# A decoder layer on one core: the last chunk's dt chain and the scan's first loads are rearranged at the seam of two stages

## The chip, the cores and the metric

The kernel runs on one core of a Trainium2 chip. Its engines are TensorE (PE, with its weight loads as PEld), VectorE (DVE), ScalarE (ACT), GpSimd (POOL) and SyncE (SP, which issues most transfers). The metric is the device time of one execution in microseconds, as the median of several runs. Before the change it is 3256.49 us (three runs, 3252.81 to 3258.94).

## The reference, cut to what matters

The input x has 4 sequences of 1024 tokens with 512 features. A Mamba block comes first, then cross-attention to 64 context tokens, then a dense layer with routed low-rank experts; each is followed by a layer norm. The change touches the Mamba block alone:

```
xz = rmsnorm(x) @ in_proj_w.T;  u, z = split(xz)          # 1024 channels each
u  = silu(causal_conv(u) + conv_b)
dt_r, Bm, Cm = split(u @ x_proj_w.T, [32, 48])            # 32, 16, 16 columns
dt = softplus(dt_r @ dt_proj_w.T + dt_proj_b)
dA = exp(dt * A);  dBu = dt * Bm * u                      # 16 states per channel
h_t = dA_t * h_{t-1} + dBu_t                              # scan over the tokens
y  = sum_n(h * Cm) + u * D;  y = y * silu(z);  out = y @ out_proj_w.T
```

All arithmetic is in f32; products that need more than the fast matmul type gives are split into a high and a low part and summed from three matmuls.

## The kernel before

**Two stages and their seam.** `mamba_in` (line 354) is the input stage. It goes through 8 chunks (`NC`) of 512 tokens (`T`). In each chunk, each of 8 slots (`KI`, `slot`, line 595) handles 128 of the 1024 channels: projection to u and z, convolution, silu. What a slot starts is finished in later slots: `at(d, phase, f)` puts a function into the table `Slots` for d slots later, and each slot runs its due functions in four phases. The table `AP` (line 33) holds the delays. The results go to DRAM: `pk[c][jp][:, :, q]` holds, for a pair of channel blocks jp, the quantities dt (q = 0), dt u (q = 1), u (2) and z (3); `b` and `c` hold B and C.

`scan_mlp` (line 658) is the second stage. Its steps (`Step`, line 681) are numbered by k: one state n of 16, for one group g of 4 channel blocks of one chunk. `load` brings in dt and dt u of a pair of blocks, `load_b` one row of B copied to all partitions, `load_c` the chunk's C. `times_b` multiplies dt u by B on GpSimd (two instructions of 128x1024 per step), `exp` makes dA on ScalarE into one of two PSUM banks (tile `da`), `scan` runs the recurrence on VectorE (four per step), `turn` transposes its result on TensorE and `times_c` multiplies by C and accumulates. `quarter(k, q, other)` (line 1095) writes out a quarter of a step: it works on steps k - 1, k and k + 1 at once. For the first 40 steps no matmuls of the following MLP run beside the scan.

**The tail of the last chunk.** When the last of a chunk's `x_proj` matmuls is issued (line 525), one slot later `project` (line 546) copies the result to `pr` (dt's input) and `bc` (B and C) on ScalarE and stores B; `project_rest` makes pr's low part on VectorE. Two slots after that `turn_c` transposes `bc` into a bank of the pool `pp`, and `put_c` (line 561) copies C out of that bank, into the first columns of `bc` itself, and stores it. The eight `dt` (line 571) follow at the delays `AP["b"]`, two in every slot from two to five slots on. Each is one matmul into one of two PSUM banks (`pd`, tile `dt`); one slot later `dt_softplus` runs on ScalarE; two slots after the second of a pair `dt_u` (line 585) stores dt, multiplies it by u on GpSimd, copies the first token's dt to `dt0` (odd chunks) and stores the product.

After the last chunk (line 645) nine more slots are written out, with no new chunk in them; what is due even later is left to the generator `rest`. Then `scan_mlp` writes step 0's loads of dt and dt u, C's load and the loads of B for steps 0 and 1, all on SyncE, then step 0's products with B and its first two exps (lines 1139 to 1148). The quarters of the first four steps (`EARLY_STEPS`) follow, and each second quarter lets `rest` run one slot more. Only then are the input stage's last pools closed (`bx.close()`) and those of the early scan opened.

**What sets the order.** Each stage issues through `InOrder` (line 294), which chains each engine's instructions, SyncE excepted, in the order in which that stage writes them. The two stages have a chain each; how the two are merged on an engine, and the order of SyncE's transfers, is decided by the framework's scheduler, which reckons with a timeline of its own. ScalarE's tables for softplus and for exp differ, so an `ACT_TABLE_LOAD` is put in wherever the two follow each other. Each transfer signals one of eight counters, taken in turn over the whole program, and is issued only when the earlier transfer on the same counter has landed; that wait stands on the engine that issues it.

Of the kernel before, what the change touches and what calls it, by code (L numbers as in the profile page):

```python
# [10 lines left out]
F32 = mybir.dt.float32  # L11
# [3 lines left out]
ALU = mybir.AluOpType  # L15
AX = mybir.AxisListType
PSUM = bass.MemoryType.PSUM
DRAM = bass.MemoryType.DRAM

P = 128  # L20
# [4 lines left out]
NS = 16  # L25
DTR = 32
T = 512
NT = T // P
NC = N // T
# [3 lines left out]
AP = {  # L33
    "cv": (1, 1),
    "cw": (1, 3),
    "ut": (2, 1),
    "uu": (2, 2),
    "up": (3, 0),
    "zt": (1, 1),
    "zz": (1, 3),  # L40
    "th": (1, 0),
# [96 lines left out]
for g, first in enumerate((4, 6)):  # L138
    for n in range(1, 16):
        for t in range(4):  # L140
            i = 4 * (n - 1) + t
# [5 lines left out]
                kind = (None, JS0, AS0, JS0, None)[i % 5]  # L147
            if kind:
                kind[g].add((n, t))
EARLY_STEPS = 4  # L150
H, DK, SK = 16, 32, 64
E, R = 8, 16
ER = E * R
# [128 lines left out]
def open_pool(tc, name, bufs, **kw):  # L282
    return tc.tile_pool(name=name, bufs=bufs, reuse_waits="tile", **kw)
# [40 lines left out]
class Slots:  # L324
# [5 lines left out]
    def at(self, d, phase, f, *args):  # L330
        self.due.setdefault((self.now + d, phase), []).append(lambda: f(*args))
# [17 lines left out]
def put(nc, dr, c, jp, q, src):  # L349

    nc.sync.dma_start(dr["pk"][c][jp][:, :, q], src)


def mamba_in(tc, cn, a, dr, sx):
# [5 lines left out]
    nc = pin  # L360
    ident, pvec = cn["ident"], cn["pvec"]
    slots = Slots()
    at, run = slots.at, slots.run
    with ExitStack() as ctx:
        up = sx.enter_context(open_pool(tc, "a_u", bufs=8, side="right"))
        pd = sx.enter_context(open_pool(tc, "a_pd", bufs=2, space=PSUM, side="right"))
        wp = ctx.enter_context(open_pool(tc, "a_w", bufs=1))
        xp = ctx.enter_context(open_pool(tc, "a_x", bufs=1))
        tp = ctx.enter_context(open_pool(tc, "a_t", bufs=2))
        sm = ctx.enter_context(open_pool(tc, "a_sm", bufs=2))  # L370
        pw = ctx.enter_context(open_pool(tc, "a_pw", bufs=2))
        qp = ctx.enter_context(open_pool(tc, "a_q", bufs=1, space=PSUM))
        pp = ctx.enter_context(open_pool(tc, "a_p", bufs=5, space=PSUM))

        wu = [wp.tile([P, KD, DI], F32R, tag=f"wu{i}", name=f"wu{i}") for i in range(2)]
# [60 lines left out]
        class Step:  # L436
# [82 lines left out]
            def x_proj(self, j):  # L519
                if j == 0:  # L520
                    self.xp = qp.tile([P, T], F32, tag="xp", name="ps_xp")
                nc.tensor.matmul(
                    self.xp, wxp[:, j], self.u[j // 2][:, j % 2], start=j == 0, stop=j == KI - 1
                )
                if j == KI - 1:
                    at(1, 0, self.project)
                    at(1, 0, self.project_rest)
                    for b in range(KI):
                        at(*AP["b"][b], self.dt, b)

            def gate(self, j):

# [20 lines left out]

            def turn_c(self):

                ps = pp.tile([P, NT, P], F32, tag="mm", name="ps_c")
                for t in range(NT):
                    nc.tensor.transpose(ps[:, t], self.bc[:, t * P : (t + 1) * P], ident)
                at(0, 1, self.put_c, ps)

            def put_c(self, ps):
                ct = self.bc[:, 0 : NT * NS].rearrange("p (t n) -> p t n", n=NS)
                nc.scalar.copy(ct, ps[:, :, 112:128])
                nc.sync.dma_start(dr["c"][self.c], ct)

# [5 lines left out]
            def dt(self, j):  # L571

                jp, i = divmod(j, 2)
                if i == 0:
                    self.dts[jp] = sp.tile([P, 2, T], F32, tag="r", name="r", bufs=4)
                ps = pd.tile([P, T], F32, tag="dt", name="ps_dt")
                nc.tensor.matmul(ps, wdt[:, j * P : (j + 1) * P], self.pr, start=True, stop=True)
                at(*AP["ds"], self.dt_softplus, j, ps, self.dts[jp][:, i])
                if i:
                    at(*AP["du"], self.dt_u, jp)  # L580

            def dt_softplus(self, j, ps, r):
                nc.scalar.activation(r, ps, AF.Softplus, bias=vec(V_DTB + j))
# [1 line left out]
            def dt_u(self, jp):  # L585
                r = self.dts.pop(jp)
                put(nc, dr, self.c, jp, 0, r)
                q = sp.tile([P, 2, T], F32, tag="q", name="q", bufs=4)
                nc.gpsimd.tensor_tensor(q, r, self.u.pop(jp), ALU.mult)
                if self.c % 2:  # L590
                    dt0 = cn["dt0"][:, self.c // 2, 2 * jp : 2 * jp + 2]
                    nc.gpsimd.tensor_copy(dt0, r[:, :, 0])
                put(nc, dr, self.c, jp, 1, q)
# [26 lines left out]
        nc = tc.nc  # L620
# [16 lines left out]
        sp = sx.enter_context(open_pool(tc, "a_sp", bufs=2, side="right"))  # L637
        nc = pin
# [3 lines left out]
                    load_in(wz, DI, j // 3, [nc.gpsimd, nc.vector])  # L642
                slot(c, j)
        assert not later
        for n in range(9):
            slot(NC, n)

    def rest():
        n = 9
        while slots.due:  # L650
            slot(NC, n)
            n += 1
            yield
# [4 lines left out]
def scan_mlp(tc, cn, a, dr, before, bx, then):  # L658
# [5 lines left out]
    nc = pin  # L664
    ident = cn["ident"]
    GJ = 4
    with ExitStack() as ctx, ExitStack() as sx:
# [6 lines left out]
        pd = sx.enter_context(open_pool(tc, "b_pd", bufs=2, space=PSUM))  # L674
# [6 lines left out]
        class Step:  # L681
# [7 lines left out]
                self.by_add, self.by_turn = (AS0[self.g], JS0[self.g]) if self.g < 2 else (AS, JS)  # L689
                self.da = {}  # L690

            def load(self, jp, q):

                pk = pks[self.g, jp, q] = kp.tile([P, 2, T], F32, tag=f"pk{q}", name=f"pk{q}")
                nc.sync.dma_start(pk, dr["pk"][self.c][2 * self.half + jp][:, :, q])

            def load_c(self):
                if self.half == 0:
                    cts[self.c] = bp.tile([P, NT, NS], F32, tag="c", name="c", bufs=2)
                    nc.sync.dma_start(cts[self.c], dr["c"][self.c])  # L700

            def load_b(self):
                bs[self.k] = bp.tile([P, 1, T], F32, tag="b", name="b")
                nc.sync.dma_start(
                    bs[self.k], dr["b"][self.c][self.n : self.n + 1].partition_broadcast(P)
                )

# [132 lines left out]
        def at(d, phase, f, *args):  # L840

            due.setdefault((now[0] + d, phase), []).append(lambda: f(*args))

        def run(phase):
            for f in due.pop((now[0], phase), ()):
                f()
# [241 lines left out]
        n = NC * 2 * NS  # L1088
# [3 lines left out]
        def step(k):  # L1092
            return all_steps[k] if 0 <= k < n else None

        def quarter(k, q, other):


            before, this, nxt = (step(i) for i in (k - 1, k, k + 1))
            run(0)
            if q == 0 and step(k + 2):  # L1100
                step(k + 2).load_b()
            after = step(k - k % NS + NS)
            if after and (k % NS, q) in LOADS:
                for jp, i in LOADS[k % NS, q]:
                    after.load(jp, i)
                if (k % NS, q) == (8, 0):
                    after.load_c()
            if after and not after.first and q == 0:
                if k % NS == 8:
                    after.first_decay()  # L1110
                elif k % NS == 9:
                    after.first_carry()
            if q == 1 and this and this.n == 12:
                this.load_uz(0, nc.sync)
                this.load_uz(1, nc.sync)
            if before:
                if q == 0:
                    before.carry()
                before.turn(q)
            run(1)  # L1120
            other()
            run(2)
            if this:
                this.scan(q)
            ahead = this if q < 2 else nxt
            if ahead:
                if q % 2 == 0 and not ahead.first:
                    ahead.carry_in(1 - q // 2)
                ahead.exp((q + 2) % GJ)
            if before:  # L1130
                before.times_c(q)
                if q == GJ - 1 and before.n == NS - 1:
                    before.end()
            if nxt and q < 2:
                nxt.times_b(q)
            run(3)
            now[0] += 1

        for jp in range(2):
            for i in range(2):  # L1140
                step(0).load(jp, i)
        step(0).load_c()
        for k in range(2):
            step(k).load_b()
        for jp in range(2):
            step(0).times_b(jp)
        for i in range(2):
            step(0).exp(i)
        for k in range(EARLY_STEPS):
            for q in range(GJ):  # L1150
                quarter(k, q, lambda: q % 2 or next(before, None))
        assert next(before, 0) == 0
        bx.close()
        with ExitStack() as zx:
            zps.append(zx.enter_context(open_pool(tc, "b_z", bufs=44, side="right")))
            zps.append(
                zx.enter_context(open_pool(tc, "b_zp", bufs=2, space=PSUM, side="right"))
            )
            for k in range(EARLY_STEPS, 2 * NS + 8):
                for q in range(GJ):  # L1160
                    quarter(k, q, lambda: None)
            turned[0] = 0
# [4 lines left out]
        pp = ctx.enter_context(open_pool(tc, "b_p", bufs=3, space=PSUM, side="right"))  # L1167
# [780 lines left out]
def build(tc, a, out):  # L1948
    nc = tc.nc
    with ExitStack() as ctx:  # L1950
# [39 lines left out]
        before = mamba_in(tc, cn, a, dr, bx)  # L1990
        att = Attention(tc, cn, a, dr, out)
        scan_mlp(tc, cn, a, dr, before, bx, lambda pin, mm: att.start(ctx, pin, mm))
        att.rest(ctx)
        att.run()
# [71 lines left out]
```

## Time and profile before

| what | us |
|---|---|
| median of three runs | 3256.49 |
| the profiled execution | 3250.26 |
| its span, first to last instruction | 3248.5 |
| VectorE busy in the span | 2698.2 (83%) |
| TensorE busy | 3001.8 (92%) |
| GpSimd busy | 2369.2 (73%) |
| ScalarE busy | 1973.4 (61%) |
| last matmul of the input stage's x_proj starts | 487.0 |
| first scan of step 0 | 508.08 |
| first scan of step 1 | 515.12 |

Times inside the execution count from the span's start. In a timeline, each row is one instruction or a run of equal ones: start, length, engine, source line, operation, tile written and tiles read; in brackets stands the engine's idle time just before it and what ended that time. Line 308 is the issuing line of `InOrder`, which nearly all instructions share, so the tiles' names tell them apart: `r` is dt, `q` is dt u, `hs` the state and before it the product with B, `da` the decay, `pr` and `bc` the projected values. Transfers are named by target and source in the same way.

### The profile page before, as it was taken

How to read it: one execution, taken by the hardware profiler on the slowest of the kernel's cores; microseconds unless marked ns; L12 is line 12 of the kernel's file. 1: busy time of each engine (PE TensorE's matmuls, PEld its weight loads, DVE VectorE, ACT ScalarE, POOL GpSimd, SP SyncE). 2: the span in 40 equal slices, each digit the busy share in tenths (PEclk: the TensorE clock that was granted, in tenths of full speed). 3: DMA queues.
4: the chain of work that ended last, by engine and by line, in shares of the span. 5: the costliest groups of instructions: out<-in, count | busy, mean ns of one | idle time of the engine just before them, and what ended most of it. 6: DMA issues, size and time to landing. Idle time of an engine off the chain costs nothing.

```text
span 3248.5 us, 47327 instructions
## 1 busy us (share of the span) xinstructions
PE 3001.8 (92%) x15992; PEld 2393.6 (74%) x15992; DVE 2698.2 (83%) x3836; ACT 1973.4 (61%) x3876; POOL 2369.2 (73%) x2169
## 2 busy tenths in 40 slices
PE   7999996887999999999999999999999997999987
PEld 5777773664876786786776786786785887898876
DVE  6876767997999999999999999999962346888876
ACT  3666666776666567666667666667642336666643
POOL 1334328998998999999999999999952115666664
PEclk9999995778999999999999999999999999999998
DMA  4778744336675775675765765765766432111110
GB/s 165 261 264 288 256 167 163 111 104 215 198 224 179 221 223 179 220 226 178 221 223 175 225 217 177 225 213 172 219 190 228 142 104 95 46 46 47 48 41 33
DMA packets 478472, 562.79 MB, mean 173 GB/s; under 512 B 46006, under 2 KB 309814, under 8 KB 477974
## 3 DMA queue, kind: packets, MB, share of 16 engines
q1 hardware_dynamic: 464406, 526.21, 50.6%
q10 hardware_dynamic: 13824, 33.56, 3.2%
q8 instruction: 127, 2.08, 0.3%
q14 instruction: 115, 0.94, 0.1%
HBM read 430.18 MB, written 129.50 MB: 172 GB/s over the span
## 4 chain that ended last, share of the span: by engine, by line
PE 34%; DVE 23%; POOL 12%; issue 8%; DMA 4%; ACT 3%; SPq 0%; ACTq 0%; DVEq 0%; POOLq 0%
DVE hs L308 10%; PE ps_ab L308 10%; POOL hs L308 6%; DVE acc L308 5%; PE ps_m L308 5%; PE ps_h L308 5%; PE ps_o L308 3%; PE ps_s L308 3%; PE ps_b L308 2%; POOL acc L308 2%; PE ps_y L308 2%; DVE g L308 1%; ACT da L308 1%; DMA uz<-pk 1%; DMA w<-w 1%
## 5 line engine op out<-in xcount | busy, mean ns | idle before, releaser
L308 DVE TENSOR_TENSOR_SCAN hs<-da,hs 128x512 f32<-128x512 f32 x1024 | 1214.7, 1207 | 42.7 <-ACT da L308 21.3
L308 POOL TENSOR_TENSOR hs<-pk,b 128x1024 f32<-128x1024 f32 x512 | 1217.2, 2393 | 29.7 <-issue 10.5
L308 ACT ACTIVATE da<-pk,aneg 128x512 f32<-128x512 f32 x1024 | 704.9, 689 | 554.3 <-DVE hs L308 548.6
L308 PE MATMUL ps_ab<-xn,w 128*128 128x512 f32 x3072 | 827.6, 406 | 0.0
L308 PE MATMUL ps_h<-ident,hs 128*128 128x128 f32 x4096 | 684.8, 292 | 91.0 <-DVE hs L308 47.3
L308 PEld LDWEIGHTS ps_h<-ident,hs 128*128 128x128 f32 x4096 | 535.5, 149 | 313.9 <-DVE hs L308 80.5
L308 PEld LDWEIGHTS ps_ab<-xn,w 128*128 128x128 f32 x3072 | 545.0, 189 | 95.8 <-issue 1.1
L308 PE MATMUL ps_m<-w,gs 128*128 128x512 f32 x1536 | 419.3, 408 | 9.5 <-POOL gs L308 9.5
L308 DVE SCALAR_TENSOR_TENSOR acc<-ps_h,c,acc 128x512 f32<-128x512 f32 x542 | 394.2, 727 | 37.8 <-PE ps_h L308 35.6
L308 POOL TENSOR_TENSOR acc<-acc,hc 128x512 f32<-128x512 f32 x232 | 300.1, 1293 | 52.9 <-ACT hc L308 51.5
L308 PEld LDWEIGHTS ps_m<-w,gs 128*128 128x128 f32 x1536 | 274.4, 191 | 61.7 <-POOL gs L308 14.5
L308 PE MATMUL ps_o<-wo,wy 128*128 128x512 f32 x512 | 247.8, 602 | 8.4 <-DMA wy<-y 5.1
L308 ACT ACTIVATE hc<-ps_h,c 128x512 f32<-128x512 f32 x344 | 231.3, 673 | 12.6 <-PE ps_h L308 12.5
L308 POOL TENSOR_TENSOR gs<-g,gs 128x512 fp32r<-128x512 f32 x128 | 165.8, 1295 | 85.1 <-ACT gs L308 85.1
L308 PE MATMUL ps_in<-xn,wu 128*128 128x512 f32 x768 | 214.7, 428 | 0.1
L308 POOL TENSOR_TENSOR pt<-pw,pt 128x512 fp32r<-128x512 f32 x48 | 62.7, 1306 | 194.9 <-ACT pt L308 131.2
L308 PE MATMUL ps_in<-xn,wz 128*128 128x512 f32 x768 | 191.8, 397 | 1.0 <-POOL wz L308 0.6
L308 PEld LDWEIGHTS ps_in<-xn,wu 128*128 128x128 f32 x768 | 145.3, 190 | 56.9 <-issue 22.0
L308 PEld LDWEIGHTS ps_in<-xn,wz 128*128 128x128 f32 x768 | 142.4, 188 | 34.8 <-POOL wz L308 1.1
L308 DVE SCALAR_TENSOR_TENSOR cv<-ps_in,pvec,cv 128x509 f32<-128x509 f32 (+2 forms) x192 | 143.3, 746 | 7.0 <-ACT cv L308 2.3
L308 ACT ACTIVATE hs<-hs,first 128x1 f32<-128x1 f32 x512 | 120.4, 284 | 27.1 <-POOL hs L308 11.7
L308 PEld LDWEIGHTS ps_o<-wo,wy 128*128 128x128 f32 x512 | 87.9, 194 | 66.5 <-issue 65.9
(244 smaller groups left out, 4623.9 us busy)
## 6 DMA issues: line engine op xcount, KB each, us to landing
w<-w SPq DMA_DIRECT2D x384, 512.0 KB, 5.6
b<-b SPq DMA_DIRECT2D x256, 256.0 KB, 4.1
pk<-pk SPq DMA_DIRECT2D x64, 512.0 KB, 6.7
w<-pt SPq DMA_DIRECT2D x48, 512.0 KB, 3.2
pk<-z SPq DMA_DIRECT2D x64, 256.0 KB, 2.9
pk<-u SPq DMA_DIRECT2D x32, 512.0 KB, 3.9
pk<-r SPq DMA_DIRECT2D x32, 512.0 KB, 3.1
pk<-q SPq DMA_DIRECT2D x32, 512.0 KB, 3.7
```

What stands on the lines that cost most here:

```text
L308: ins = f(*args, **kw)
```

## The change

Five things are done. The last chunk's eight dt no longer keep the delays of `AP["b"]`: pair by pair they are due in the slots two to five after `x_proj`'s end, each softplus in the same slot as its matmul and each `dt_u` in that slot as well. In the last chunk `dt_u` multiplies on VectorE instead of GpSimd; the copy to `dt0` stays on GpSimd. Step 0's loads are issued by ScalarE, B first, then dt u of both pairs, then dt of both, then B of step 1, and step 0's products with B are written directly after them, ahead of the tail; C's load stays on SyncE. Only three slots are written before the scan's pools are opened; the rest of the tail is written out in one go after the products, and the exps of step 0 and all quarters follow it, so `EARLY_STEPS` goes. C gets its own tile `ct` in every chunk instead of the first columns of `bc`, and in the last chunk its transposes use a dt bank; the pool of x_proj's bank moves to the outer stack, as it now lives longer.

```diff
-EARLY_STEPS = 4
+        qp = sx.enter_context(open_pool(tc, "a_q", bufs=1, space=PSUM, side="right"))
...
-        qp = ctx.enter_context(open_pool(tc, "a_q", bufs=1, space=PSUM))
...
-                        at(*AP["b"][b], self.dt, b)
+                        at(*(AP["b"][b] if self.c < NC - 1 else (2 + b // 2, 0)), self.dt, b)
...
-                ps = pp.tile([P, NT, P], F32, tag="mm", name="ps_c")
+                if self.c < NC - 1:
+                    ps = pp.tile([P, NT, P], F32, tag="mm", name="ps_c")
+                else:
+                    ps = pd.tile([P, NT, P], F32, tag="dt", name="ps_c")
...
-                ct = self.bc[:, 0 : NT * NS].rearrange("p (t n) -> p t n", n=NS)
+                ct = sp.tile([P, NT, NS], F32, tag="ct", name="ct", bufs=1)
...
-                at(*AP["ds"], self.dt_softplus, j, ps, self.dts[jp][:, i])
+                ds, du = (AP["ds"], AP["du"]) if self.c < NC - 1 else ((0, 1), (0, 2))
+                at(*ds, self.dt_softplus, j, ps, self.dts[jp][:, i])
                 if i:
-                    at(*AP["du"], self.dt_u, jp)
+                    at(*du, self.dt_u, jp)
...
-                nc.gpsimd.tensor_tensor(q, r, self.u.pop(jp), ALU.mult)
+                eng = nc.gpsimd if self.c < NC - 1 else nc.vector
+                eng.tensor_tensor(q, r, self.u.pop(jp), ALU.mult)
...
-        for n in range(9):
+        for n in range(3):
             slot(NC, n)
...
-        n = 9
+        n = 3
...
-            def load(self, jp, q):
+            def load(self, jp, q, eng=nc.sync):
...
-            def load_b(self):
+            def load_b(self, eng=nc.sync):
...
-        for jp in range(2):
-            for i in range(2):
-                step(0).load(jp, i)
+        step(0).load_b(nc.scalar)
+        for i in (1, 0):
+            for jp in range(2):
+                step(0).load(jp, i, nc.scalar)
+        step(1).load_b(nc.scalar)
         step(0).load_c()
-        for k in range(2):
-            step(k).load_b()
         for jp in range(2):
             step(0).times_b(jp)
+        for _ in before:
+            pass
         for i in range(2):
             step(0).exp(i)
-        for k in range(EARLY_STEPS):
-            for q in range(GJ):
-                quarter(k, q, lambda: q % 2 or next(before, None))
-        assert next(before, 0) == 0
         bx.close()
...
-            for k in range(EARLY_STEPS, 2 * NS + 8):
+            for k in range(2 * NS + 8):
```

More of the change, by code (lines that the diff above doesn't have):

```diff
@@ L690, in __init__ @@
                 self.da = {}
-            def load(self, jp, q):
+            def load(self, jp, q, eng=nc.sync):
                 pk = pks[self.g, jp, q] = kp.tile([P, 2, T], F32, tag=f"pk{q}", name=f"pk{q}")
-                nc.sync.dma_start(pk, dr["pk"][self.c][2 * self.half + jp][:, :, q])
+                eng.dma_start(pk, dr["pk"][self.c][2 * self.half + jp][:, :, q])
             def load_c(self):
@@ L700, in load_c @@
                     nc.sync.dma_start(cts[self.c], dr["c"][self.c])
-            def load_b(self):
+            def load_b(self, eng=nc.sync):
                 bs[self.k] = bp.tile([P, 1, T], F32, tag="b", name="b")
-                nc.sync.dma_start(
+                eng.dma_start(
                     bs[self.k], dr["b"][self.c][self.n : self.n + 1].partition_broadcast(P)
```

## The prediction

> **What bounds the kernel now.** I read the page's slices first: in the eighth of them (569 to 650 us and on) VectorE is full, in the seventh (487 to 569) it is not. The change touches only the seam there between two stages: the end of the input stage (last eight dt blocks) and the first steps of the scan. So I cut the span into stretches around it. Columns: stretch, its length, then busy us (and instructions) of PE, PEld, DVE, ACT, POOL, then granted clock, DMA share, GB/s.
>
> ```profile
> 490.00:500.00 10.00, 4.73 (x10) 2.43 (x10) 0.00 (x0) 5.95 (x9) 4.38 (x3) 0.50 0.99 347
> 510.00:520.00 10.00, 5.33 (x19) 3.55 (x19) 7.60 (x8) 5.84 (x12) 10.00 (x7) 0.50 0.73 259
> 520.00:530.00 10.00, 7.47 (x31) 5.70 (x30) 10.00 (x11) 6.50 (x13) 10.00 (x5) 0.50 0.16 55
> ```
>
> From 520 us VectorE and GpSimd work without a gap, and VectorE stays at 9.3 us or more of every 10 up to 740 us (one stretch of 8.3). So a shift of the point where VectorE starts to run steadily reaches the end of the stage at full size; nothing behind the seam is changed. That point is the third row of VectorE's timeline (start, length, instruction, idle before it and what ended it):
>
> ```profile
> 489.17 0.68 DVE L308 TENSOR_TENSOR pr<-ps_xp,pr 32x512 fp32r<-32x512 f32 x1 [3.26 <-ACT bc L308]
> 508.08 4.64 DVE L308 TENSOR_TENSOR_SCAN hs<-da,hs 128x512 f32<-128x512 f32 x4 [18.23 <-POOL hs L308]
> 515.12 5.84 DVE L308 TENSOR_TENSOR_SCAN hs<-da,hs 128x512 f32<-128x512 f32 x5 [2.40 <-POOL hs L308]
> ```
>
> Step 0's scans (508.08) start 18.23 us after VectorE's last work of the input stage, and step 1's (515.12) wait again for GpSimd. GpSimd's timeline says what it did:
>
> ```profile
> 503.28 2.35 POOL L308 TENSOR_TENSOR q<-r,u 128x1024 f32<-128x1024 f32 x1 [2.72 <-issue]
> 505.71 4.64 POOL L308 TENSOR_TENSOR hs<-pk,b 128x1024 f32<-128x1024 f32 x2
> 510.31 2.34 POOL L308 TENSOR_TENSOR q<-r,u 128x1024 f32<-128x1024 f32 x1
> 512.74 13.91 POOL L308 TENSOR_TENSOR hs<-pk,b 128x1024 f32<-128x1024 f32 x6
> ```
>
> The products of step 0 wait behind the third dt u, those of step 1 (512.74) behind the fourth. The dt's come from ScalarE:
>
> ```profile
> 484.19 0.63 ACT L308 ACTIVATE u<-cv 128x512 f32<-128x512 f32 x1
> 488.07 0.58 ACT L308 CAST pr<-ps_xp 96x512 fp32r<-96x512 f32 x1 [3.25 <-PE ps_xp L308]
> 490.77 1.28 ACT L308 ACT_TABLE_LOAD   x1 [1.63 <-issue]
> 492.07 1.27 ACT L308 ACTIVATE r<-ps_dt,pvec 128x512 f32<-128x512 f32 x2
> 496.57 0.21 ACT L308 COPY bc<-ps_c 128x64 f32<-128x64 f32 x1 [3.24 <-DMA b<-bc]
> 496.68 1.27 ACT L308 ACTIVATE r<-ps_dt,pvec 128x512 f32<-128x512 f32 x2
> 497.97 1.28 ACT L308 ACT_TABLE_LOAD   x1
> 499.27 1.30 ACT L308 ACTIVATE da<-pk,aneg 128x512 f32<-128x512 f32 x2
> 500.58 1.28 ACT L308 ACT_TABLE_LOAD   x1
> 501.88 1.27 ACT L308 ACTIVATE r<-ps_dt,pvec 128x512 f32<-128x512 f32 x2
> 503.50 1.26 ACT L308 ACTIVATE r<-ps_dt,pvec 128x512 f32<-128x512 f32 x2 [0.36 <-issue]
> ```
>
> Eight softplus (r), two exps of step 0 (da), a table load wherever the two alternate, and 3.24 us lost because C is copied into B's tile while B's transfer still reads it. Lastly the transfers between 478 and 520 us (KB each, median us to landing): they are slow here because the DMA engines are full.
>
> ```profile
> pk<-pk SPq DMA_DIRECT2D x6, 512.0 KB, 7.8
> pk<-u SPq DMA_DIRECT2D x1, 512.0 KB, 3.6
> c<-c SPq DMA_DIRECT2D x2, 32.0 KB, 7.4
> ```
>
> **The change, step by step.** The measure is the start of step 1's products on GpSimd: 512.74 now, that is 24.67 us after ScalarE's pr copy at 488.07.
>
> *ScalarE from pr on, in the changed program's order.* Call pr's start 0. Up to the end of the first two softplus nothing differs: 5.27 (492.07 + 1.27 - 488.07). The C copy no longer stands there, so the second pair follows at the spacing of the last two pairs now (503.50 - 501.88 = 1.62): 5.62 to 6.89. C's transpose now takes a dt bank: it starts when that is free (6.26), 1.05 us on PE, copy 0.21, done at 7.7; the fifth dt matmul stands behind it (0.7), so the fifth softplus runs 8.1 to 8.75. Then the order alternates: table load, two exps (11.35), table load, two softplus (13.9), table load, two exps (16.5), table load, eighth softplus (18.45), at 1.30 us a load (499.27 - 497.97), 1.30 two exps, 1.27 two softplus. That is five loads on the path where there are three now. GpSimd's small dt0 copy (0.19) and then step 1's products: 18.65. Against 24.67 this is **-6.0 us**, in which removing C's wait (3.24) and the dt u from GpSimd outweigh two more loads (2.6).
>
> *Table loads, rule against row.* The row shows a change of tables costing 1.30 us with no gap behind it. The Trainium skill (ScalarE: Activation LUTs, What ACT_TABLE_LOAD costs) gives about 1.28 us plus a drain of about 1.38 us for each switch; by it the two further loads would cost 5.3 us instead of 2.6, and the net below would be 1.3 us of loss, where the row gives a gain. I take the row.
>
> *The dt u on VectorE.* No row has it. Nearest is u, also from two SBUF operands, 128x512: 0.69 us with GpSimd idle, 1.08 beside its work; so 1.3 to 2.1 us for each 128x1024, four of them 5.2 to 8.4. I take 1.7. The first two (at 5.3 and 6.9) fall where VectorE is idle; the third (13.9 to 15.6) ends before the second pair of exps (15.9); the fourth (18.45 to 20.2, at worst 20.6) ends before GpSimd's first product of step 1 (18.65 + 2.35 = 21.0). Cost 0; with that cover gone the fourth costs up to 2.1.
>
> *Step 0's products right then.* On GpSimd they stand behind the last dt u of the chunk before (done 485.4) and wait for B and dt u loads alone: about 491 to 496, where they start at 505.71 now. Step 0's scans, now bounded by exps, start at 10.75 after pr. Nothing waits for them longer than counted.
>
> *The loads on ScalarE's queue, ahead of pr.* This is the cost. In the program every transfer signals one of eight counters in turn and first waits for the transfer eight before it; today SP pays for such waits. Six triggers (0.33 us each, like ScalarE's y stores later) now stand on ScalarE between u (484.19) and pr, and pr cannot pass them. Their waits: B none; dt u of block 0 none, so both go by 484.9; dt u of block 1 for an r store issued at 482.91 (3.1 us: 486.0); dt of block 0 for the store of the last u, issued at 485.94; dt of block 1 for the load of C, issued by SP at 486.5; B of step 1 for the dt u load of 484.6. The u store lands after 3.6 us now (489.5), but with 1.25 MB of loads beside it at the 400 GB/s of this stretch (up to 3 us): 491.5. C: 2.8 (its store, page) to 7.4 us: about 492. The dt u load: 6.7 us (page): 491.3. So the last trigger leaves near 492.4 and pr runs at 492.7 instead of 488.07: **+4.6 us**. Bounds: all at their quickest (u 3.6 us, then three triggers) 490.6, +2.5; all at 8.5 us, the slowest store of this stretch, 495.7, +7.6. If the waits were met in time, 0. I take the middle as the queue is full: the 490 row has a DMA share of 0.99.
>
> *The trigger side, rule.* The Trainium skill (DMA: Bandwidth & Descriptors, Issuing engines are not separate DMA queues) says that another issuing engine saves issue time only. The rows agree that bandwidth is the limit here (403 GB/s from 500 to 510 us).
>
> *SP.* It sheds six triggers; prefetches (u and z, blocks 2 and 3) move ahead of the last stores and take DMA time from them, but those stores are read only much later. B of steps 2 and 3 is issued before it is due. *The tail drained before step 0, the first steps' pools opened early, C's own tile in the other chunks, the softplus bank's move:* no row shows a wait on them (C's copy at 461.55 has none); 0, bound 0.5 either way.
>
> Sum: -6.0 + 4.6 = **-1.4 us**. Profiled execution: 3250.26 us, span 3248.5; it would be 3248.9. The median of the runs shown is 3256.49, 6.2 above the profiled one; on it: **3255.1**.
>
> **Rivals.** *A, ScalarE hardly waits:* then -6.0, 3250.5. For it: the first three triggers' counters are met by 486.0, and pr must wait for PE until 488.07 anyway. Against: the u store cannot be down before 489.5.
> *B, slower: the stall eats the gain.* Place: ScalarE's fourth to sixth trigger; price 7.6 - 6.0 = +1.6 us, 3258.1. It decides once pr comes more than 6.0 us late, at 494.1. For it: median landings of 7 to 8 us in this stretch. Against: they belong to a backlog that builds up only after 488.
> *C, the dt's do not follow each other:* the two exps between them are in the program, and counted; if the last two softplus waited for step 0's scans a further round (two exps and a load, 2.6), +1.2.
> *D, something I do not see:* PE's granted clock is 0.50 here and changes later; a moved clock could add or take some us.
>
> **How the numbers follow.** Forecast (net between -4 and +1.3, C in it) 0.62, A 0.15, B 0.13, D 0.10. 0.2% is 6.5 us; the three runs shown spread over 6.1 us, so 0.2% is about what can be told from no change. A alone comes near that bound: half of it, with the scatter, and half of D make faster 0.12; half of D and a fifth of B slower 0.08; the same 0.80. Range: A less 3.5 us of scatter, B plus 3.9: 3247 to 3262.
>
> **What would show it.** ScalarE's pr at 490.6 to 495.7 with its idle time ended by a DMA; GpSimd's first hs near 491; no idle of 3.24 at C's copy; six table loads; step 1's first scan near 513.8. Wrong: pr at 488 (A), a stall beyond 8 us, or VectorE idle after step 1 behind a dt u.

## The result, and the profile after

The changed kernel takes 3257.14 us (median of 22 runs, 3251.33 to 3262.71) where the kernel before takes 3252.52 (22 runs, 3249.16 to 3259.3). The ratio is 1.0012, with a 95% interval of 1.0006 to 1.0017: slower by about 3.9 us, between 2.0 and 5.5 (the two medians alone stand 4.6 apart). The forecast was 1.4 us of gain; set on these 22 runs of before, that would have been 3251.1. 3257.14 lies inside the range, which at 15 us is wide enough to hold a gain and a loss, but on the other side of before. What came is rival B, a stall at ScalarE's triggers that eats the gain, and the stall was larger than the bound set for it.

The profiled execution took 3260.21 us, its span 3258.4. Its input stage ended 2.6 us later than in the profile of before. That differs from one execution to the next and is not the change: the later time is there already at the first chunk's `pr` copy (97.33 us against 94.49), and two kernels run below that share the input stage's edits have 94.48 and 94.49 there; from the first chunk's `pr` to the seventh's it is 345.6 us after and 345.8 before. So from here on times at the seam are counted from one event that the change doesn't touch, U, the end of VectorE's last `u` of the input stage: 485.90 before, 488.50 after. Its rows, before and after:

```profile
484.85 1.05 DVE L308 SCALAR_TENSOR_TENSOR u<-u,cv 128x512 f32<-128x512 f32 x1 [2.23 <-ACT u L308]
```

```profile
487.45 1.05 DVE L307 SCALAR_TENSOR_TENSOR u<-u,cv 128x512 f32<-128x512 f32 x1 [2.23 <-ACT u L307]
```

ScalarE's timeline of the changed kernel (start, length, instruction, idle before it and what ended it; ACTq are transfers that ScalarE issues):

```profile
484.76 0.35 ACTq L307 DMA_DIRECT2D b<-b  x1
...
485.15 0.59 ACTq L307 DMA_DIRECT2D pk<-pk  x1
...
486.78 0.63 ACT L307 ACTIVATE u<-cv 128x512 f32<-128x512 f32 x1
492.70 5.22 ACTq L307 DMA_DIRECT2D pk<-pk  x3
497.96 0.92 ACTq L307 DMA_DIRECT2D b<-b  x1
498.93 0.58 ACT L307 CAST pr<-ps_xp 96x512 fp32r<-96x512 f32 x1 [11.52 <-DMA pk<-pk]
...
506.44 0.21 ACT L307 COPY ct<-ps_c 128x64 f32<-128x64 f32 x1 [0.62 <-PE ps_c L307]
506.91 0.69 ACT L307 ACTIVATE r<-ps_dt,pvec 128x512 f32<-128x512 f32 x1 [0.27 <-PE ps_dt L307]
507.62 1.28 ACT L307 ACT_TABLE_LOAD   x1
508.91 1.30 ACT L307 ACTIVATE da<-pk,aneg 128x512 f32<-128x512 f32 x2
...
516.72 0.69 ACT L307 ACTIVATE r<-ps_dt,pvec 128x512 f32<-128x512 f32 x1
```

The first two triggers go at once. The third leaves only at 492.70, the sixth near 498, and `pr` at 498.93: 10.4 us after U, where before it was 2.2 us after U. The 3.24 us of idle before C's copy are gone, and the table loads among softplus and exp still stand next to their neighbours with 0.01 to 0.02 us between them (the first one behind `pr` follows 1.64 us of idle, as it did 1.63 before).

The transfers say for whom the third and fourth trigger waited. These are the stores that SyncE issued at 485.50 (`r`) and 488.52 (`u`), each from its own stretch of the list of transfers (KB, us from issue to landing):

```profile
pk<-r SPq DMA_DIRECT2D x1, 512.0 KB, 7.2
```

```profile
pk<-u SPq DMA_DIRECT2D x1, 512.0 KB, 8.2
```

485.50 + 7.2 = 492.70, to the hundredth the start of the third trigger. 488.52 + 8.2 = 496.7, and the fourth, which is inside the row of three above, left at 496.74. Before, the same two stores took 3.1 and 3.6 us.

The trace also says where the `r` store's time went. These are all the packets of the 3.1 us after its issue, by DMA queue (packets, MB, share of the 16 engines; q1 carries SyncE's transfers, q10 ScalarE's), before (482.9 to 486) and after (485.5 to 488.6):

```profile
q1 hardware_dynamic: 374, 0.73, 63.3%
```

```profile
q10 hardware_dynamic: 264, 0.51, 72.0%
```

Before, SyncE's stores moved, with the first packet 1.16 us after the `r` store's issue. After, only the two loads from ScalarE's queue moved, and the first packet of SyncE's queue came at 488.75, 3.25 us after that store's issue. In the other four kernels with loads on ScalarE it came 3.0 to 3.3 us after the issue as well.

The stretches around the seam (columns as in the prediction's first fence: length, busy us and instructions of PE, PEld, DVE, ACT and POOL, granted clock, DMA share, GB/s):

```profile
490.00:500.00 10.00, 0.00 (x0) 0.00 (x0) 0.00 (x0) 1.06 (x2) 2.34 (x1) 0.50 1.04 343
500.00:510.00 10.00, 5.60 (x11) 2.68 (x11) 3.45 (x4) 7.08 (x10) 2.72 (x3) 0.50 1.03 384
510.00:520.00 10.00, 4.13 (x13) 2.56 (x13) 6.83 (x6) 9.88 (x13) 3.78 (x3) 0.50 0.88 269
520.00:530.00 10.00, 5.39 (x20) 3.69 (x20) 8.96 (x9) 7.00 (x15) 10.00 (x5) 0.50 0.32 96
```

From 490 to 500 us almost nothing is computed (before, ScalarE was busy for 5.95 us of it, PE for 4.73), while the DMA engines are full. GpSimd, full from 510 on before, is so from 520 on. VectorE's and GpSimd's timelines show what became of the rest:

```profile
504.28 1.24 DVE L307 TENSOR_TENSOR q<-r,u 128x1024 f32<-128x1024 f32 x1 [3.57 <-ACT r L307]
...
517.44 1.23 DVE L307 TENSOR_TENSOR q<-r,u 128x1024 f32<-128x1024 f32 x1 [0.20 <-ACT r L307]
521.04 5.84 DVE L307 TENSOR_TENSOR_SCAN hs<-da,hs 128x512 f32<-128x512 f32 x5 [2.38 <-POOL hs L307]
```

```profile
491.39 2.34 POOL L307 TENSOR_TENSOR hs<-pk,b 128x1024 f32<-128x1024 f32 x1 [3.44 <-DMA pk<-pk]
501.07 2.35 POOL L307 TENSOR_TENSOR hs<-pk,b 128x1024 f32<-128x1024 f32 x1 [7.34 <-DMA pk<-pk]
504.25 0.19 POOL L307 COPY dt<-r 128x2 f32<-128x2 f32 x1 [0.83 <-ACT r L307]
...
517.46 1.25 POOL L307 COPY dt<-r 128x2 f32<-128x2 f32 x1 [3.95 <-ACT r L307]
518.66 9.28 POOL L307 TENSOR_TENSOR hs<-pk,b 128x1024 f32<-128x1024 f32 x4
```

Step 1's products start at 518.66, which is 19.73 us after `pr` (24.67 before). The dependent work did become shorter; it starts too late. The table compares landmarks, in us from U (step 1's first scan is VectorE's fifth scan; the first `hz` is a ScalarE instruction some 26 us further into the scan; the first y store is one of ScalarE's; the x store is SyncE's at about 1065 us of the span):

| | pr | step 1's first scan | first hz | first y store | x store |
|---|---|---|---|---|---|
| before | 2.2 | 29.2 | 55.1 | 130.0 | 579.1 |
| after | 10.4 | 32.5 | 58.4 | 133.2 | 584.1 |

The 3.3 us of the seam reach the y store unchanged. By the x store they are 5.0. The stretch between those two stores took 449.1 us before, 450.9 after, and 448.8 to 451.1 in the other kernels run below, the quickest ones at the seam included; so the last 1.7 us can't be told from what that stretch does by itself, and what moves it stays open.

### The profile page after: what moved, and what is told of

Its sections match the earlier page's. It is cut to its first block, busy times and chain, and to the rows that moved or that the text cites. A ratio compares the mean times of both kernels' runs of the same rounds, so it can differ in the third digit from the quotient of the medians.

```text
span 3258.4 us, 47312 instructions
## 1 busy us (share of the span) xinstructions
PE 2996.8 (92%) x15992; PEld 2391.2 (73%) x15992; DVE 2704.7 (83%) x3840; ACT 1976.4 (61%) x3878; POOL 2362.4 (73%) x2165
## 3 DMA queue, kind: packets, MB, share of 16 engines
q8 instruction: 127, 2.08, 0.3%
## 4 chain that ended last, share of the span: by engine, by line
PE 36%; DVE 22%; POOL 11%; issue 8%; DMA 4%; ACT 3%; SPq 0%; ACTq 0%; DVEq 0%; POOLq 0%
PE ps_ab L307 10%; DVE hs L307 10%; PE ps_m L307 6%; POOL hs L307 5%; DVE acc L307 5%; PE ps_h L307 5%; PE ps_o L307 4%; PE ps_s L307 3%; PE ps_b L307 2%; POOL acc L307 2%; DVE g L307 1%; PE ps_y L307 1%; DMA uz<-pk 1%; ACT da L307 1%; PE ps_num L307 1%
## 5 line engine op out<-in xcount | busy, mean ns | idle before, releaser
L307 ACT ACTIVATE hc<-ps_h,c 128x512 f32<-128x512 f32 x344 | 231.3, 673 | 11.1 <-PE ps_h L307 11.0
```

The lines of the kernel that those rows point to most:

```text
L307: ins = f(*args, **kw)
```

## The experiments

Two things had to be separated: why `pr` is late, and what the rest of the change is worth without that.

**The loads back on SyncE.** The edit, in the changed kernel:

```diff
-        step(0).load_b(nc.scalar)
+        step(0).load_b()
...
-                step(0).load(jp, i, nc.scalar)
-        step(1).load_b(nc.scalar)
+                step(0).load(jp, i)
+        step(1).load_b()
```

> Step 0's loads and B of step 1 are issued by SyncE instead of ScalarE; all else as in the changed kernel (the scheduler then puts all eight softplus ahead of the exps). M is the time from the end of VectorE's last u to step 1's first scan: 29.2 us before the change, 32.5 after it. Theory W (the loss is ScalarE waiting for other transfers before it may issue): pr starts about 2.2 us after u's end as before the change, the chain from pr to step 1's scan is 17.7 us, M = 20 to 22, time 7 to 9 us below the kernel before, ratio 0.997 to 0.998. Rival T (the transfers are crowded, whoever issues them): the products or exps of step 0 then wait for their loads, M stays at 29 or more, ratio 1.000 to 1.002.

Measured: 3250.71 us, ratio 0.9997 (0.9988 to 1.0006). At the seam it came as the theory of ScalarE's wait at the triggers says: `pr` 1.2 us after U, step 1's first scan 20.6.

```profile
488.37 0.58 ACT L307 CAST pr<-ps_xp 96x512 fp32r<-96x512 f32 x1 [2.30 <-PE ps_xp L307]
```

In this program the scheduler also put all eight softplus ahead of the exps, which leaves two table loads where the changed kernel has six. The total missed the expected 0.997 to 0.998: the first `hz` is at 51.5, only 3.6 us ahead of before, and the total shows no more than that. GpSimd's timeline shows where 5 us were given back:

```profile
503.28 9.27 POOL L307 TENSOR_TENSOR hs<-pk,b 128x1024 f32<-128x1024 f32 x4
519.77 4.63 POOL L307 TENSOR_TENSOR hs<-pk,b 128x1024 f32<-128x1024 f32 x2 [7.22 <-PE ps_h L307]
```

Step 3's products wait 7.22 us. The profile names PE, but B of step 3 is the likelier one: SyncE issues it only at 508.52, behind the stores of dt and dt u and four prefetches, and it lands after 11.1 us, at 519.6.

```profile
b<-b SPq DMA_DIRECT2D x1, 256.0 KB, 11.1
```

**One chain for both stages, the loads still on ScalarE.** This forces all eight softplus ahead of the exps:

```diff
-    return rest()
+    return rest(), pin.last
...
-    pin = InOrder(tc, tc.nc)
+    pin = InOrder(tc, tc.nc, last)
```

> The changed kernel with one order for both stages on every engine (the scan's chain goes on where the input stage's ends), so that all eight softplus stand before the exps; the loads stay on ScalarE. Theory W plus three table loads less: pr still 10 to 11 us after u's end, then 17.7 us instead of 22.1 to step 1's first scan, M = 28, ratio 0.9997 to 1.0001. Rival (the alternation of softplus and exp is hidden): M = 32.5, ratio 1.0012.

Measured: 3252.02 us, ratio 0.9999 (0.9989 to 1.0008). The stall stays, as expected, and everything behind it is shorter:

```profile
496.48 0.58 ACT L307 CAST pr<-ps_xp 96x512 fp32r<-96x512 f32 x1 [10.74 <-DMA pk<-pk]
...
504.46 1.31 ACT L307 ACTIVATE r<-ps_dt,pvec 128x512 f32<-128x512 f32 x2 [0.26 <-PE ps_dt L307]
506.09 1.27 ACT L307 ACTIVATE r<-ps_dt,pvec 128x512 f32<-128x512 f32 x2 [0.32 <-POOL dt L307]
507.38 1.28 ACT L307 ACT_TABLE_LOAD   x1
508.67 1.30 ACT L307 ACTIVATE da<-pk,aneg 128x512 f32<-128x512 f32 x2
```

`pr` is at 9.7, step 1's first scan at 27.2 instead of 32.5, the first `hz` at 52.1. So the alternation of softplus and exp, which the changed kernel leaves to the scheduler, costs about 4.6 us at step 1 (5.3 less the 0.7 by which `pr` was earlier). The softplus now run without exps between them, and of the six table loads behind `pr` two are left; three of the four lay on the path to step 1, 3.9 us at 1.30 each.

**dt u back on GpSimd in the last chunk.**

```diff
-                eng = nc.gpsimd if self.c < NC - 1 else nc.vector
+                eng = nc.gpsimd
```

> The changed kernel with the last chunk's dt u back on GpSimd. Theory: the fourth dt u (2.35 us) and the dt0 copy (0.19) then stand between the last softplus and step 1's products, where the changed kernel has a copy of 1.25 alone: M = 33.8 instead of 32.5, ratio about 1.0016. Rival (dt u on VectorE delays the scans more than it frees GpSimd): M below 32, ratio below 1.0012.

Measured: 3254.85 us, ratio 1.0012 (1.0003 to 1.0021). Step 1's first scan is at 33.8 instead of 32.5, with `pr` at the same 10.4. So moving dt u to VectorE is worth 1.3 us at the seam; in the total, 1.3 us can't be told from nothing.

**dt0's copies on VectorE as well.**

```diff
-                    nc.gpsimd.tensor_copy(dt0, r[:, :, 0])
+                    eng.tensor_copy(dt0, r[:, :, 0])
```

> The changed kernel with the dt0 copies on VectorE, so that nothing on GpSimd waits for the last softplus. Theory: step 1's products follow step 0's at once, and step 1's first scan waits for ScalarE's exp and VectorE's fourth dt u instead, about 20.5 us after pr where it is 22.1 now: M = 31, ratio 1.0007. Rival (the products were not what step 1 waited for): M = 32.5, ratio 1.0012.

Measured: 3256.45 us, ratio 1.0013 (1.0004 to 1.0022); step 1's first scan at 31.4 and `pr` at 10.0, so 0.7 us gained behind `pr` and nothing in the total: a miss for the total. GpSimd is released from the copies, but step 1's products did not follow step 0's at once: they waited until 507.26 for B of step 1, the sixth of ScalarE's loads (5.38 us of idle, ended by that transfer). Then they run beside VectorE's part, which stretches (VectorE's timeline):

```profile
504.14 1.23 DVE L307 TENSOR_TENSOR q<-r,u 128x1024 f32<-128x1024 f32 x1 [0.32 <-issue]
505.28 0.16 DVE L307 COPY dt<-r 128x2 f32<-128x2 f32 x1
...
510.48 2.50 DVE L307 TENSOR_TENSOR q<-r,u 128x1024 f32<-128x1024 f32 x1 [0.20 <-ACT r L307]
512.91 2.30 DVE L307 COPY dt<-r 128x2 f32<-128x2 f32 x1
```

**Only the first two loads on ScalarE.** Two readings of the stall were left: that ScalarE waits at its triggers, or that the crowd of transfers itself, or the issuing, holds everything. And it was open what makes the stores slow. The edit, with the one chain of above:

```diff
-                step(0).load(jp, i, nc.scalar)
-        step(1).load_b(nc.scalar)
+                step(0).load(jp, i, nc.scalar if i and jp == 0 else nc.sync)
+        step(1).load_b()
```

> The changed kernel with one chain for both stages (so that all eight softplus come before the exps, as in the run of the chain alone), and only the first two of the six loads (B, dt u of block 0, whose waits are met when they are reached) on ScalarE; the other four go to SyncE. If pr is late because ScalarE's third to sixth trigger wait for stores of SyncE (theory): pr at +1.2 to +2.2 from the end of VectorE's last u, instead of +9.7, with no idle time ended by a transfer, although the r and u stores may still land late; step 1's first scan at 19 to 21. For what makes the stores slow: if the two loads issued ahead of them are enough, the last r and u stores land after 5 us or more; if only all six make them slow, after 4 us or less, as with no load on ScalarE (3.1 and 3.3). Rival, a transfer's issue itself holds ScalarE, whatever its wait: pr at +4 or later. B of step 3 is issued late here too, so the first hz at 50 to 53 and a ratio of 0.9985 to 1.0000.

Measured: 3250.08 us, ratio 0.9992 (0.9982 to 1.0001). ScalarE's timeline:

```profile
484.26 0.34 ACTq L307 DMA_DIRECT2D b<-b  x1
...
484.64 0.59 ACTq L307 DMA_DIRECT2D pk<-pk  x1
...
489.19 0.58 ACT L307 CAST pr<-ps_xp 96x512 fp32r<-96x512 f32 x1 [2.30 <-PE ps_xp L307]
```

The transfers issued between 484.4 and 485.5, and the one after 487:

```profile
pk<-r SPq DMA_DIRECT2D x1, 512.0 KB, 8.4
```

```profile
pk<-u SPq DMA_DIRECT2D x1, 512.0 KB, 7.1
```

The stores are as slow as in the changed kernel, and `pr` is on time, 1.2 us after U, released by PE. So the two things are separate. Two loads issued just ahead (0.75 MB) are enough to make the stores slow; what makes `pr` late (9.7 us after U with all six loads there and the same chain) is that triggers which must wait for those stores stand ahead of it on its engine. Step 1's first scan is at 19.6, the first `hz` at 50.2, since B of step 3 is late here too (GpSimd idle 6.53 us, ended by B's transfer by the profile's own word).

**The same six triggers on GpSimd.** Its next work is the products of these very loads, so a wait there would cost less. With the one chain, and B of steps 2 and 3 issued early by SyncE (four tiles for B):

```diff
-                bs[self.k] = bp.tile([P, 1, T], F32, tag="b", name="b")
+                bs[self.k] = bp.tile([P, 1, T], F32, tag="b", name="b", bufs=4)
...
-            if q == 0 and step(k + 2):
-                step(k + 2).load_b()
+            if q == 0 and k and step(k + 3):
+                step(k + 3).load_b()
...
-        step(0).load_b(nc.scalar)
+        step(0).load_b(nc.gpsimd)
...
-                step(0).load(jp, i, nc.scalar)
-        step(1).load_b(nc.scalar)
+                step(0).load(jp, i, nc.gpsimd)
+        step(1).load_b(nc.gpsimd)
+        for k in range(2, 4):
+            step(k).load_b()
```

> The changed kernel with one chain for both stages, its six loads on GpSimd's queue instead of ScalarE's, and B of steps 2 and 3 issued early by SyncE (four tiles for B). The same waits then stand on an engine whose next work is the products of these very loads. Theory: pr at +1.2 to +2.2 from the end of VectorE's last u; the six triggers leave as late as on ScalarE (the sixth near +9 to +10), the dt loads land at +17 to +20, so step 0's exps wait for them rather than for softplus; step 1's first scan at 21 to 24, first hz at 47 to 50, ratio 0.9975 to 0.9985. Rival, what delays pr is the crowd of transfers and not the queue that it stands behind: pr at +6 or later here too, step 1's first scan at 27 or later, ratio about 0.9995 to 1.0005.

Measured: 3247.48 us, ratio 0.9980 (0.9971 to 0.9989): faster than both kernels. GpSimd's timeline:

```profile
486.04 0.77 POOL L307 DMA_DIRECT2D b<-b  x1
486.82 2.86 POOL L307 DMA_DIRECT2D pk<-pk  x4
489.68 0.55 POOL L307 DMA_DIRECT2D b<-b  x1
494.02 5.64 POOL L307 TENSOR_TENSOR hs<-pk,b 128x1024 f32<-128x1024 f32 x2 [3.79 <-DMA pk<-pk]
499.62 3.57 POOL L307 COPY dt<-r 128x2 f32<-128x2 f32 x4
503.14 13.91 POOL L307 TENSOR_TENSOR hs<-pk,b 128x1024 f32<-128x1024 f32 x6
```

`pr` is 2.2 us after U, step 1's first scan at 20.9, the first `hz` at 45.8. Expectations missed: the triggers did not leave as late as on ScalarE but one after the other, the last by 490.2, and with them the loads of dt landed earlier (11.1 and 13.0 us after U, not 17 to 20) and the first `hz` came before 47. In the program each of GpSimd's six transfers signals a counter of its own, which no other transfer uses, so these triggers wait for no store; the trace agrees, as all six had left by 490.2 while the `u` store landed only at 492.0 (486.68 + 5.3). They only cost GpSimd 0.55 to 0.77 us each. The stall was thus not merely moved to an engine where it's cheap. It did not arise.

**The loads on SyncE with B early.** The first run's edit and the lines on B of the last one, with B of steps 1 to 3 issued right behind step 0's loads:

```diff
-        step(1).load_b()
+        for k in range(1, 4):
+            step(k).load_b()
```

> The kernel with step 0's loads on SyncE, plus four tiles for B instead of three, with B of steps 1 to 3 issued together with step 0's loads and every later B three steps ahead instead of two. Times from U, the end of VectorE's last u. If the part that the first such run gave back (its gain shrank from 8.6 us at step 1's first scan to 3.6 us at the first hz) is the late B of step 3 alone: pr at +1.2, step 1's first scan at 20.6, no idle time of GpSimd at step 3's products, first hz at 46.5 to 48 (before: 55.1), and a ratio to the kernel before of 0.9974 to 0.998. Rival, the transfers are only too many, so that an earlier B moves the wait to another load: step 1's first scan 2 us or more later than 20.6, or a gap of GpSimd of 3 us or more within steps 1 to 4, first hz at 50 or more, ratio 0.9985 or more.

Measured: 3246.01 us, ratio 0.9983 (0.9974 to 0.9992), also faster than both kernels. GpSimd's timeline:

```profile
502.74 13.90 POOL L307 TENSOR_TENSOR hs<-pk,b 128x1024 f32<-128x1024 f32 x6
516.59 1.27 POOL L307 TENSOR_TENSOR acc<-acc,hc 128x512 f32<-128x512 f32 x1
520.51 4.67 POOL L307 TENSOR_TENSOR hs<-pk,b 128x1024 f32<-128x1024 f32 x2 [2.65 <-DMA b<-b]
```

`pr` 1.2, step 1's first scan 20.5, no wait at step 3's products (they are the last two of the six), first `hz` at 47.1, inside the 46.5 to 48 expected. So the late B of step 3 was what the first run gave back; 2.65 us of waiting remain for B of step 4. The ratio lies just outside the 0.9974 to 0.998 expected: 8.1 us ahead at the y store, 7.1 at the x store, about 5.5 (2.6 to 8.5) in the total. Between this kernel and the one with the loads on GpSimd the ratios can't tell: their intervals overlap almost wholly.

All together, in us from U:

| | pr | step 1's first scan | first hz | first y store | x store | ratio |
|---|---|---|---|---|---|---|
| before | 2.2 | 29.2 | 55.1 | 130.0 | 579.1 | 1 |
| after | 10.4 | 32.5 | 58.4 | 133.2 | 584.1 | 1.0012 |
| dt u on GpSimd | 10.4 | 33.8 | 59.7 | 134.5 | 585.1 | 1.0012 |
| dt0's copies on VectorE | 10.0 | 31.4 | 56.3 | 131.2 | 582.3 | 1.0013 |
| one chain | 9.7 | 27.2 | 52.1 | 127.0 | 575.9 | 0.9999 |
| loads on SyncE | 1.2 | 20.6 | 51.5 | 126.4 | 575.2 | 0.9997 |
| two loads on ScalarE, one chain | 1.2 | 19.6 | 50.2 | 125.5 | 575.1 | 0.9992 |
| loads on SyncE, B early | 1.2 | 20.5 | 47.1 | 121.9 | 572.0 | 0.9983 |
| loads on GpSimd, one chain, B early | 2.2 | 20.9 | 45.8 | 120.7 | 571.6 | 0.9980 |

Where nothing stalls, `pr` is at 2.2 before and with the loads on GpSimd, and at 1.2 in three others; PE ended the idle time in both cases, after 3.25 and 2.30 us. That microsecond is TensorE's clock: the last two x_proj matmuls took 2.08 us before and with the loads on GpSimd, where the granted clock was 0.50 (486 to 488 us before), and 1.12 to 1.14 us in the three, with a clock of 1.00 (487.2 to 488.2 us with the loads on SyncE). Both clocks occur among the kernels with the change, so about 1 us of the seam's gain in the three rows with 1.2 is the clock's.

In seven of the eight kernels the total is worse against before than the first y store says, by 0.7 to 3.0 us (9.3 us ahead there and 6.5 in the total for the last row). The intervals of the totals are about that wide and every row is held against the same one profile of before, so this may be chance; what else it could be was not looked for.

## Why the prediction was wrong, step by step

**The step that failed is "The loads on ScalarE's queue, ahead of pr", +4.6 us with bounds of +2.5 and +7.6.** It measured 10.43 - 2.17 = +8.3 us from U. The mechanism was read rightly, down to which trigger waits for which transfer. The place of the first two triggers, and with it the landings, were wrong. The step took the r store at 3.1 us, as before, and concluded that the first three triggers' waits were met by 486.0; and it took the u store at 5.6 us, adding 2 us for loads beside it. Measured, they took 7.2 and 8.2. The step let the first two loads go behind ScalarE's `u` (484.19), by 484.9, and so 1.3 us or more behind the `r` store of 482.91. In the program they went ahead of that `u`, 0.74 and 0.35 us ahead of the `r` store (484.76 and 485.15 against 485.50), and the store was priced without them: the 3.1 us come from a profile in which nothing is queued there. In the runs this is plain: 3.1 us for r and 3.3 for u with no load ahead (loads on SyncE); 8.4 and 7.1 with only those two ahead; and with GpSimd's loads, which come between the two stores as the prediction had it, 3.1 for r and 5.3 for u, close to its 3.1 and 5.6. The 384 GB/s of the second row above would carry 0.75 MB in 2 us, but the store lost 4 to 5: SyncE's queue did not move while the two loads did, and from 486 to 488 they moved at 187 GB/s alone. Why the one queue stood and why the loads were no quicker isn't shown by a row and stays open.

The upper bound held the landing itself, with 8.5 us for the u store. It failed on the triggers behind it, priced at 0.33 us each: from 496.7 the last three took until 498.88, 0.7 each. So `pr` came 10.4 us after U, 0.6 beyond the +9.8 that the bound stood for (495.7 - 485.9).

**"ScalarE from pr on", -6.0 us:** measured 19.73 - 24.67 = -4.9. The order was as written, with five table loads between `pr` and the last softplus, which ended 18.48 us after `pr` (18.45 predicted). The missing 1.1 us is GpSimd's last dt0 copy, priced at 0.19 from the rows of before: it took 1.25, because the dt u that had moved to VectorE ran beside it. The change itself made that row invalid.

So the sum at step 1's products was +8.3 - 4.9 = +3.3 us (8.26 - 4.94), and not -1.4, and 3.3 us is what the scan, the `hz` and the y store show.

**"The dt u on VectorE", 1.3 to 2.1 us, taken 1.7, cost 0:** 1.23 us each, just under the lower bound, since no product of GpSimd ran beside them; the last ended at 518.67, before the end of GpSimd's first product of step 1, as said. Beside GpSimd's products it would have been dearer: 2.50 us in the run with dt0's copies on VectorE, and 2.1 to 3.4 over all runs where one of GpSimd's products had started first, at or above the upper bound.

**"Table loads, rule against row":** the row held. Four of the chain's five loads stand 0.01 to 0.02 us from their neighbours, and the first has the same idle time before it as before the change; the further drain of about 1.38 us that the Trainium skill (ScalarE: Activation LUTs, What ACT_TABLE_LOAD costs) gives does not show here. An estimate from that page makes the chain 5 x 1.38 = 6.9 us longer than it was.

**"The trigger side, rule":** the last four loads took 8.2 to 10.1 us on ScalarE's queue, no quicker than on SyncE's before (7.3 to 8.2 for dt and dt u), in agreement with the rule; the first two, sent when the DMA engines were idle, took 4.8 and 6.1. What it does not price is that loads on one queue held up a store on the other, as shown above, and the wait at the trigger. The Trainium skill says elsewhere (DMA: Bandwidth & Descriptors, Anatomy of one DMA) that a transfer's wait stands on the sequencer that issues it; the 11.52 us of idle time before `pr`, against 2.30 when only the two triggers with waits already met stand there, are what that costs here.

**"Step 0's products right then":** the first at 491.39, near 491 as said; the second only at 501.07, because the third trigger was late. Step 0's scans did not wait for it: the first started at 509.70, behind ScalarE's exp.

**"SP", "B of steps 2 and 3 is issued before it is due":** true in the changed kernel only because its seam is late. Where `pr` is on time, B of step 3 holds GpSimd for 7.2 us. **The other edits costed at nothing** (C's tile in the other chunks, the early pools) show no wait in the trace after, and the way from the first chunk's `pr` to the seventh's took no longer than before (345.6 against 345.8 us, as above). C's tile alone was not run.

**Rival A** (no stall) would have fallen short of its -6.0 as well: the chain alone gives -4.9. Where the stall was taken away the gain at step 1 was larger, 8.6, but that includes a better order of softplus and exp and the microsecond of TensorE's clock, and more than half of it is lost again to the late B. **Rival C** did not occur beyond what was counted. **Rival D** was not needed: TensorE's clock did differ (the last two x_proj matmuls took 1.19 us after and 2.08 before), but `pr` waited for transfers by then.

## What to carry to other kernels

Before a load is moved to a computing engine's queue, list what each trigger will wait for, look where in that engine's order the trigger will stand, and price the landings of those transfers with the moved loads already in the DMA engines, not as the trace of before has them; here 3.1 and 3.6 us became 7.2 and 8.2, and the engine's critical instruction stood behind them. With the same six loads on GpSimd, whose transfers had counters of their own and whose next work needed them, an early B and one fixed order, the kernel was 6.5 us (3.6 to 9.4) faster than before. With the loads left on SyncE and an early B it was 5.5 us (2.6 to 8.5) faster, which can't be told from that; so nothing here shows that these loads gain by leaving SyncE. And a stage that starts sooner needs its later loads sooner too: 5 of 8.6 us went back to one row of B until its load was issued earlier.

## What the runs showed of the hardware that was not expected

A 512 KB store of SyncE took 3.1 to 3.6 us with no load ahead of it. It took 7.2 and 8.4 when 0.75 MB of loads from ScalarE's queue had been issued less than a microsecond ahead, and the store behind it 8.2 and 7.1. In the changed kernel only ScalarE's queue moved for the first 3.1 us of that store.

A small GpSimd copy (128x2) took 0.18 to 0.19 us alone, and also when it started just ahead of VectorE's product of two SBUF operands (504.25 against 504.28). It took 1.24 to 1.25 when it started just behind one, ending when that ended (517.46 + 1.25 = 518.71 against 517.44 + 1.23 = 518.67); four of them took 3.57 us in the run with the loads on GpSimd. The other way round, VectorE's dt u took 1.23 us alone and 2.1 to 3.4 where one of GpSimd's products had started first. Once, in the run with one chain, it started 0.11 us ahead of such a product: it took 1.23 and the product 3.33 instead of 2.34. The Trainium skill (GPSIMD Engine Reference, Specifications) says that GpSimd shares its SBUF interfaces with VectorE and that instructions of VectorE with two SBUF inputs contend for them; these rows agree.
